# An attention stage on one NeuronCore: the token selection moved beside the next image's queries, and feature squares and products spread over ScalarE and GpSimd

## The chip, the core and the metric

The kernel runs on one core of one Trainium2 chip. A core has five engines that run their own instruction streams and meet at semaphores: TensorE (PE in the profile; its weight loads are listed apart as PEld), VectorE (DVE), ScalarE (ACT), GpSimd (POOL) and SyncE (SP, which here only issues transfers). The metric is the device time of one execution in microseconds, and it is compared by the median of several executions.

## The reference, cut to what matters

The input is four images of 256 channels and 56x56 positions, in float32. A first layer (group norm and a 7x7 involution) writes `x`. The second layer treats the 3136 positions of an image as tokens of 256 numbers:

```
t = tokens(x)
# attention, 8 heads of 32:  the weight of a pair is a square, not an exponential
scores = q . k * 32**-0.5
p      = (scores + 5)**2
t      = t + proj(sum_m p[n,m] v[m] / sum_m p[n,m])
# half of the tokens go through an MLP
u      = layernorm(t)
w      = u . wr + br
pick the 1567 tokens of largest w  (ties: lower index first)
t      = t + u  and, for the picked ones,  + w * (gelu(u @ w1 + b1) @ w2 + b2)
```

Because the weight is a polynomial of second degree in `q . k`, the sum over `m` needs no 3136x3136 matrix: it is a linear function of the 528 products `k_i k_j` of a head, of the 32 `k_i` and of a constant, each summed with `v` over all tokens.

## The kernel before, in words

`conv_layer` takes the first 1890 us of the profile and is not touched. `attn_ffn_layers` follows; nearly every instruction of it passes through `InOrder` (line 849), which keeps an engine's instructions in the order in which the program issues them. The exceptions before the change are the GpSimd instructions of this function, which are issued by `nc.gpsimd` itself and may be reordered by the framework.

For each image `b` (four of them) the program does this:

- `keys(b, g)` for the two groups of four heads, `g` = 0 and 1. It goes over the tokens in 25 tiles `m` of 128. `tokens(m)` multiplies a tile of normalised tokens `xn` with the K and V weights into PSUM (`pv`), and ScalarE copies `k` twice into one of five rows buffers `ls`, and `v` into its own tile. `features(m)` makes the products: one VectorE instruction writes `phi` (128 x 4 heads x 512: `k` times `k` shifted by 0 to 15 places; shift 0 gives the squares), a second one writes the 4x16 products of shift 16 into `ls`. `add(m, phi)` multiplies `v` with `phi` and `ls` and adds up in PSUM (`accs`, `accq`). The program issues `features(m)`, then `add(m - 1)`, then `tokens(m + 3)`.
- `coefficients(b, g)`: turns the sums into matrices for the queries, in five steps (VectorE arithmetic on `accs`/`accq`, then small matmuls and transposes `pl`, `pt`, `pr`, `pd`, each read by VectorE).
- `project(b, q)`: makes the queries `qT` of a chunk `q` of 448 tokens (seven chunks in an image) and their squares `q2`.
- `queries(b)`: 7 chunks x 2 groups x 4 feature blocks = 56 steps. In a step TensorE makes products (`pg`), ScalarE squares them (`ph`), and TensorE adds up the block of the step before (`acc`). 

All else hangs on these two loops as side work: `later` is a list of Python generators, `aside()` advances each of them by one `yield`, and `run(...)` calls `aside()` after each step of `keys` or `queries`. So a generator's `yield` sets how many steps lie between two of its parts. In the list are `weigh` (denominators), `normalise(b + 1, q)` (layer norm of the next image, which fills its `xn`), `divide` and `tokens_out` (the attention output of a chunk, its layer norm into `rows`, then two GpSimd instructions of 112x1024: `uw` for the router weights and `tk` for the residual; two steps later VectorE reduces `uw` to `w`), and `select(b)`.

`select(b)` finds the 1567 largest of the 3136 weights `w`. It builds the threshold four bits at a time: `reaching` compares all weights with up to 15 trial values on VectorE (`hit`, `per`), and after a `yield` one small matmul `pn` sums over partitions; VectorE turns the result into the next digit (`good`, `digit`, `bits`, `base`). That is done nine times, then a few matmuls (`pm`, `pa`, `pb`) give each token its place, and 28 indirect transfers by GpSimd (`us`, line 1463) scatter the rows to DRAM, two a step; each of them waits for the one before. `select(b)` enters `later` when the last chunk of image `b` is done, which is in the first part of `keys(b + 1, 0)`; for the last image it runs beside the MLP (from about 3580 us).

PSUM tiles that matter: `mm` (2 buffers, for `pv` and `pg`), `acc` (2 buffers), `sm` (2 buffers, for every small matmul: `mean`, `var`, `pq`, `pu`, `pn`, `po`, and those of `coefficients` and `select`). A buffer is free again when its last reader is done.

Before the change the order between the loops is written so:

```
        later.append(project(b, 0))
        for _ in range(5):
            aside()
        run(queries(b))
```

so that `coefficients(b, 1)` and the first queries are complete before the first step of `queries(b)`.

Of the kernel before, what the change touches and what calls it, by code (L numbers as in the profile page):

```python
# [15 lines left out]
P = 128  # L16
# [845 lines left out]
def attn_ffn_layers(  # L862
# [31 lines left out]
    sm = ctx.enter_context(tc.tile_pool(name="attn_sm", bufs=2, space=PSUM))  # L894

    inner = ctx.enter_context(ExitStack())
    xnp = inner.enter_context(tc.tile_pool(name="xn", bufs=2))
    kp = inner.enter_context(tc.tile_pool(name="k", bufs=3))
    php = inner.enter_context(tc.tile_pool(name="phi", bufs=2))
    cp = inner.enter_context(tc.tile_pool(name="coef", bufs=2))  # L900
    stp = inner.enter_context(tc.tile_pool(name="sums", bufs=1))
    qp = inner.enter_context(tc.tile_pool(name="q", bufs=2))
    ve, te, se, sy = (
        InOrder(tc, e) for e in (nc.vector, nc.tensor, nc.scalar, nc.sync)
    )

    par = const.tile([P, len(COLS)], F32, name="apar")
# [54 lines left out]
        lss.append(ls)  # L962

    QUARTERS = [slice(h * DH, (h + 1) * DH) for h in range(4)]
    xns, held, later = {}, {}, []

    def load(b, q, tag):
        t = tp.tile([P, 2, CH], F32, tag=tag, name=f"{tag}{b}_{q}")
# [5 lines left out]
    def normalise(b, q):  # L974

        t = load(b, q, "t")
        yield
        p = sm.tile([P, 512], F32, tag="sm", name=f"mean_{b}_{q}")
        for c in range(2):
            te.matmul(p[:, :CH], mean_w, t[:, c], start=c == 0, stop=c == 1)  # L980
        xc = xns[b][:, :, q * CH : (q + 1) * CH]
        ve.tensor_tensor(xc, t, p[:, :CH].unsqueeze(1).to_broadcast([P, 2, CH]), ALU.subtract)
        sq = lnp.tile([P, 2, CH], F32, tag="sq", name=f"sq_{b}_{q}", bufs=1)
        se.activation(sq, xc, AF.Square)
        yield

        n = CH // 4
        p = sm.tile([P, 512], F32, tag="sm", name=f"var_{b}_{q}")
        for c in range(2):
            for j, r in enumerate(QUARTERS):  # L990
                te.matmul(
                    p[r, :n], mean_w[:, :DH], sq[:, c, j * n : (j + 1) * n],
                    start=c == 0, stop=c == 1, skip_group_check=True,
                )
# [24 lines left out]

    def keys(b, g):  # L1020

        xn = xns[b]
# [26 lines left out]
        def features(m):  # L1049

            mn = size(m)
            ls, k = lss[m % NKV], ks.pop(m)
            phi = php.tile([P, 4, NF], F32, tag="phi", name=f"phi_{b}_{g}_{m}")
            ve.tensor_tensor(
                phi[:mn].rearrange("p h (l e) -> p h l e", e=DH),
                k.unsqueeze(2).to_broadcast([mn, 4, HALF, DH]),
                further(ls[:mn, :, HALF : HALF + DH], HALF), ALU.mult,
            )
            ve.tensor_tensor(
                ls[:mn, :, :HALF], k[:, :, :HALF], ls[:mn, :, DH : DH + HALF], ALU.mult  # L1060
            )
            return phi

# [115 lines left out]
    def project(b, q):  # L1179

        f = slice(q * CH, (q + 1) * CH)
        qT = qp.tile([P, 2, CH], F32, tag="qT", name=f"qT_{b}_{q}")
        q2 = qp.tile([P, 2, CH], F32, tag="q2", name=f"q2_{b}_{q}")
        held["q", b, q] = qT, q2
        for g in range(2):
            p = sm.tile([P, 512], F32, tag="sm", name=f"pq{g}_{b}_{q}")
            for c in range(2):
                te.matmul(
                    p[:, :CH], wqkv[:, c, g * P : (g + 1) * P], xns[b][:, c, f],
                    start=c == 0, stop=c == 1,  # L1190
                )
            ve.tensor_scalar(qT[:, g], p[:, :CH], col(f"q_{g}"), SCALE, ALU.add, ALU.mult)
            nc.gpsimd.tensor_tensor(q2[:, g], qT[:, g], qT[:, g], ALU.mult)  # L1193
            yield

    def weigh(b, q, g):
# [114 lines left out]
    def tokens_out(b, q, both):  # L1311

        t = load(b, q, "tr")
        if q == 0:
            held["rows", b] = slp.tile([TB, NTB, ROW_N], F32, tag="rows", name=f"rows_{b}")
            held["w", b] = slp.tile([TB, NTB], F32, tag="w", name=f"w_{b}", bufs=2)
        rows = held["rows", b][:, q * 4 : q * 4 + 4]
        u = rows[:, :, :C]
# [40 lines left out]
        nc.gpsimd.tensor_tensor(uw, u, wr.to_broadcast([TB, 4, C]), ALU.mult)  # L1359
        nc.gpsimd.tensor_tensor(tk, tk, u, ALU.add)  # L1360
        yield
        yield
        w = held["w", b][:, q * 4 : q * 4 + 4]
# [3 lines left out]
            out[b, q * CH : (q + 1) * CH].rearrange("(j p) c -> p j c", p=TB), tk  # L1367
        )
        if q == NCH - 1:
            later.append(select(b))  # L1370

    def select(b):

# [6 lines left out]
        def reaching(values, n, at):  # L1380

            hit = slp.tile([TB, 15, NTB], F32, tag="hit", name=f"hit_{b}_{at}")
            ve.tensor_tensor(
                hit[:, :n], w.unsqueeze(1).to_broadcast([TB, n, NTB]),
                values.unsqueeze(2).to_broadcast([TB, n, NTB]), ALU.is_ge,
            )
            per = slp.tile([TB, 15], F32, tag="per", name=f"per_{b}_{at}", bufs=2)
            ve.tensor_reduce(per[:, :n], hit[:, :n], AX.X, ALU.add)
            yield
            held["reaching"] = count(n, f"pn{at}")  # L1390
            te.matmul(held["reaching"], ones, per[:, :n], start=True, stop=True)

# [4 lines left out]
        base = small(1, "base", I32)  # L1397
        yield from reaching(zero, 1, "sign")
        ve.tensor_scalar(base, held.pop("reaching"), float(TOPK), -1.0, ALU.is_lt, ALU.mult)
        yield  # L1400
        for i, shift in enumerate(SHIFTS):
            n = 15 if i else 7
            tried = slp.tile([TB, 15], I32, tag="tried", name=f"tried_{b}_{i}", bufs=2)
            ve.tensor_tensor(
                tried[:, :n], digits[:, i, :n], base.to_broadcast([TB, n]), ALU.bitwise_xor
            )
            yield from reaching(tried.bitcast(F32)[:, :n], n, i)
            good = slp.tile([TB, 15], F32, tag="good", name=f"good_{b}_{i}", bufs=2)
            ve.tensor_scalar(good[:, :n], held.pop("reaching"), float(TOPK), None, ALU.is_ge)
            digit = slp.tile([TB, 1], F32, tag="digit", name=f"digit_{b}_{i}", bufs=2)  # L1410
            ve.tensor_reduce(digit, good[:, :n], AX.X, ALU.add)
            bits = slp.tile([TB, 1], I32, tag="bits", name=f"bits_{b}_{i}", bufs=2)
            ve.tensor_scalar(bits, digit, float(1 << shift), None, ALU.mult)
            ve.tensor_tensor(base, base, bits, ALU.bitwise_xor)
            yield
        least = base.bitcast(F32)

        def standing(of, name):
# [7 lines left out]
            te.matmul(p, before, of, start=True, stop=False)  # L1426
            te.matmul(p, sums, before[:NTB, :NTB], start=False, stop=True)
            held["standing"] = p

        more, equal = small(NTB, "more"), small(NTB, "equal")  # L1430
        ve.tensor_scalar(more, w, least, None, ALU.is_gt)
# [3 lines left out]
        yield  # L1435
        p = count(1, "pm")
        te.matmul(p, ones, per, start=True, stop=True)
        room = small(1, "room")
        ve.tensor_scalar(room, p, -1.0, float(TOPK), ALU.mult, ALU.add)
        yield  # L1440
# [19 lines left out]
        ve.tensor_scalar(own_at, number, float(b * HW), None, ALU.add)  # L1460
        yield
        for m in range(NTB):
            nc.gpsimd.indirect_dma_start(  # L1463
                us[b], bass.IndirectOffsetOnAxis(ap=to[:, m : m + 1], axis=0), rows[:, m], None
            )
            if m % 2:
# [6 lines left out]
        for _ in steps:  # L1473
            aside()

    xns[0] = xnp.tile([P, 2, HW], F32, tag="xn", name="xn_0")
    for q in range(NCH):
        f = slice(q * CH, (q + 1) * CH)
        sy.dma_start(xns[0][:, :, f], ln0.rearrange("(c p) f -> p c f", p=P)[:, :, f])
    for b in range(NB):  # L1480
        if b + 1 < NB:
            xns[b + 1] = xnp.tile([P, 2, HW], F32, tag="xn", name=f"xn_{b + 1}")
        for g in range(2):
            run(keys(b, g))
            later.append(coefficients(b, g))
            aside()
        later.append(project(b, 0))
        for _ in range(5):
            aside()
        run(queries(b))  # L1490

    inner.close()
# [54 lines left out]
    def second(i):  # L1547
# [10 lines left out]
        for m in range(0, k, 2):  # L1558
# [10 lines left out]
            for j in range(2):  # L1569
# [4 lines left out]
                nc.gpsimd.indirect_dma_start(  # L1574
                    out.rearrange("b n c -> (b n) c"),
                    bass.IndirectOffsetOnAxis(
                        ap=rows.bitcast(I32)[:, m + j, C + 1 : C + 2], axis=0
# [170 lines left out]
```

## Time and profile before

| | |
|---|---|
| median of 3 executions | 3981.64 us (3970.96 to 3990.05) |
| profiled execution | 3992.79 us, span of its instructions 3991.0 us |
| mean granted TensorE clock | 0.946 of full speed |
| TensorE busy | 3586.3 us (90%), VectorE 2653.2 us (66%), ScalarE 1872.8 us (47%), GpSimd 1805.3 us (45%) |
| first layer | 0 to about 1890 us |
| attention, images 0 to 3 | about 1890 to 3570 us |
| MLP on the picked tokens | about 3580 to 3991 us |

Instructions are named in the profile as output tile <- input tiles, with the buffers' numbers left out. Almost all carry line 849, which is the helper's; so they are told apart by their tiles. A row of the table of windows gives the busy time of each engine in a stretch (union of its instructions), the granted clock of TensorE, and the share of the transfer engines. A row of the waits names who waited, for whom, how long in total, how often and the longest. The busy time of TensorE is modelled at its ends, so that 100% busy does not mean that it ran at its peak.

### The profile page before, as it was taken

To read this page: it belongs to the slowest core of one execution; us is meant where nothing else is said; L and a number is where in the kernel's file an instruction comes from. 1 tells how busy PE (TensorE), PEld (TensorE's weight loads), DVE (VectorE), ACT (ScalarE), POOL (GpSimd) and SP (SyncE) were. 2 spreads that over 40 slices of the span, in tenths; PEclk is the share of its full clock that TensorE was granted. 3 is DMA by queue.
4 is the path that set the end of the run, shared out by engine and by line. 5 is a ranking of instruction groups with operands and counts; after the bars stand their busy time and mean duration, and the time that the engine had idled before them with its cause. 6 is when DMAs were issued, how large, how long until landed. Compare 5 with 4: busy or idle time off the path is not lost.

```text
span 3991.0 us, 60965 instructions
## 1 busy us (share of the span) xinstructions
PE 3586.3 (90%) x23248; PEld 1629.9 (41%) x23248; DVE 2653.2 (66%) x3611; ACT 1872.8 (47%) x3837; POOL 1805.3 (45%) x856
## 2 busy tenths in 40 slices
PE   3989998999799999997889878998889878989998
PEld 1333333333233333332434444344434444436776
DVE  2688888899688988997954577346834576333321
ACT  2767766776477756772234412442134312442111
POOL 1568886888688978995001102111122103112231
PEclk7989999999799999998999979998899979999999
DMA  3666556664756546654002201221012201121120
GB/s 95 153 140 148 123 140 155 143 137 96 159 125 136 122 100 131 129 113 117 7 18 62 62 10 32 54 60 38 15 45 60 54 6 36 39 79 38 45 59 25
DMA packets 337515, 329.95 MB, mean 83 GB/s; under 512 B 68606, under 2 KB 327894, under 8 KB 337222
## 3 DMA queue, kind: packets, MB, share of 16 engines
q1 hardware_dynamic: 322428, 302.52, 33.9%
q0 software_dynamic: 8064, 19.48, 1.6%
q10 hardware_dynamic: 6730, 4.05, 0.4%
q8 instruction: 183, 3.00, 0.3%
q14 instruction: 110, 0.90, 0.1%
HBM read 256.77 MB, written 68.69 MB: 82 GB/s over the span
## 4 chain that ended last, share of the span: by engine, by line
PE 71%; DVE 16%; DMA 6%; issue 3%; ACT 1%; POOL 1%; SPq 1%; ACTq 0%; DVEq 0%; POOLq 0%
PE acc L849 19%; PE p L849 17%; PE pg L849 5%; DVE phi L849 5%; PE py L849 5%; PE pv L849 4%; PE ph L849 4%; PE po L849 4%; PE accs L849 3%; DVE pr L849 3%; PE z L849 3%; PE pq L849 2%; DMA xc<-x3d 1%; DVE st L849 1%; PE mean L849 1%
## 5 line engine op out<-in xcount | busy, mean ns | idle before, releaser
L849 POOL TENSOR_TENSOR pr<-xc,lg 128x1792 f32<-128x1792 f32 x280 | 1035.2, 3704 | 285.2 <-ACT lg L849 102.7
L849 PE MATMUL acc<-pr,same 128*32 128x448 f32 (+1 forms) x5824 | 682.4, 562 | 71.4 <-DVE pr L849 59.3
L849 PE MATMUL p<-y,cw 128*128 128x400 f32 (+5 forms) x1568 | 684.6, 541 | 2.4 <-ACT y L849 1.5
L849 ACT ACTIVATE ph<-pg,unit 128x896 f32<-128x896 f32 x448 | 426.8, 1004 | 462.9 <-PE pg L849 462.6
L849 DVE TENSOR_TENSOR pr<-xc,exp 128x1792 f32<-128x1792 f32 x280 | 559.4, 1998 | 54.7 <-DMA xc<-x3d 30.5
L849 DVE TENSOR_TENSOR phi<-pv,ls 128x2048 f32<-128x2048 f32 (+1 forms) x200 | 456.7, 2284 | 12.8 <-ACT v L849 10.3
L849 ACT ACTIVATE y<-p,tb,bn2s 128x200 f32<-128x200 f32 (+1 forms) x728 | 342.3, 520 | 229.4 <-PE p L849 225.2
L849 PEld LDWEIGHTS p<-y,cw 128*128 128x128 f32 (+1 forms) x1568 | 267.4, 192 | 403.1 <-issue 206.9
L849 DVE TENSOR_TENSOR pr<-xw,exp 128x1792 f32<-128x1792 f32 x168 | 338.4, 2015 | 42.3 <-issue 14.3
L849 ACT ACTIVATE ls<-pv 128x256 f32<-128x256 f32 (+1 forms) x200 | 77.5, 387 | 604.2 <-issue 510.2
L849 PE MATMUL pv<-wqkv,xn 128*128 128x256 f32 (+1 forms) x800 | 255.0, 448 | 99.5 <-DVE ls L849 73.5
L1359 POOL TENSOR_TENSOR uw<-rows,awr 112x1024 f32<-112x1024 f32 x28 | 66.0, 2359 | 601.5 <-DVE rows L849 601.5
L849 POOL TENSOR_TENSOR y<-a,ac 128x896 f32<-128x896 f32 x168 | 277.6, 1653 | 129.0 <-DMA ac<-x3d 98.0
L1463 POOL DMA_INDIRECT us<-rows,to x112 | 106.2, 948 | 487.1 <-DVE rows L849 288.9
L849 PEld LDWEIGHTS acc<-pr,same 128*32 128x32 f32 (+1 forms) x5824 | 145.5, 110 | 432.8 <-issue 245.2
L849 PE MATMUL pg<-qT,pairs 32*128 32x448 f32 x1792 | 282.5, 590 | 8.4 <-ACT ph L849 7.9
L849 PE MATMUL accs<-phi,v 128*32 128x512 f32 (+1 forms) x1600 | 235.9, 664 | 38.3 <-DVE phi L849 22.8
L1193 POOL TENSOR_TENSOR q<-qT 128x448 f32<-128x448 f32 x56 | 58.6, 1046 | 424.9 <-DVE qT L849 386.2
L849 ACT ACTIVATE lg<-p,par 128x448 f32<-128x448 f32 x392 | 233.4, 595 | 5.8 <-PE p L849 5.7
L849 PE MATMUL acc<-ph,cf 128*32 128x448 f32 (+1 forms) x1792 | 214.8, 551 | 0.0
L849 PEld LDWEIGHTS pv<-wqkv,xn 128*128 128x128 f32 (+1 forms) x800 | 153.9, 213 | 144.9 <-issue 99.7
L849 ACT ACTIVATE lg<-lg 128x1120 f32<-128x1120 f32 x168 | 163.9, 1007 | 99.1 <-DVE lg L849 98.5
(246 smaller groups left out, 5210.0 us busy)
## 6 DMA issues: line engine op xcount, KB each, us to landing
xw<-x3d SPq DMA_DIRECT2D x224, 248.0 KB
xq<-in_x SPq DMA_DIRECT2D x47, 448.0 KB
xc<-x3d SPq DMA_DIRECT2D x54, 248.0 KB
xc<-x3d SPq DMA_DIRECT2D x54, 247.0 KB
xc<-x3d SPq DMA_DIRECT2D x54, 246.0 KB
xc<-x3d SPq DMA_DIRECT2D x54, 245.0 KB
xr<-in_x SPq DMA_DIRECT2D x224, 56.0 KB
xs<-xr SPq DMA_DIRECT2D x224, 56.0 KB
```

Of the source, the lines that this page charges most:

```text
L849: return lambda *a, **k: self.tc.keep_in_program_order(of(*a, **k))
L1193: nc.gpsimd.tensor_tensor(q2[:, g], qT[:, g], qT[:, g], ALU.mult)
L1359: nc.gpsimd.tensor_tensor(uw, u, wr.to_broadcast([TB, 4, C]), ALU.mult)
L1463: nc.gpsimd.indirect_dma_start(us[b], bass.IndirectOffsetOnAxis(ap=to[:, m : m + 1], axis=0), rows[:, m], None)
```

## The change

- `select(b)` of the first three images goes to a list `whole`, and joins `later` only when `keys(b + 1, 1)` is over. It then runs beside `queries(b + 1)`. `rows` of even images take the memory that a second `xn` had, since two of them now live at once; there is one `xn` for all images.
- In `select` a `yield` now follows each counting matmul, and the one after the arithmetic goes: matmul and reader are a step apart.
- `project(b, 0)` moves from behind the keys into `keys(b, 1)`. The five bare `aside()` calls go, so that `coefficients(b, 1)` is advanced once after the keys and then by the steps of `queries(b)`.
- `features(m)`: ScalarE writes the squares (shift 0: 4 heads x 32, so 128 of the 2048 elements of `phi` in each partition) from `ls`; VectorE's instruction covers the other 1920; GpSimd writes the 4x16 products from `ls`.
- The squares `q2` of the queries go from GpSimd to ScalarE.
- GpSimd's instructions of this function are now kept in program order (`gp`).

```diff
-    xnp = inner.enter_context(tc.tile_pool(name="xn", bufs=2))
+    xnp = inner.enter_context(tc.tile_pool(name="xn", bufs=1))
...
-    ve, te, se, sy = (
-        InOrder(tc, e) for e in (nc.vector, nc.tensor, nc.scalar, nc.sync)
+    ve, te, se, sy, gp = (
+        InOrder(tc, e) for e in (nc.vector, nc.tensor, nc.scalar, nc.sync, nc.gpsimd)
     )
...
             phi = php.tile([P, 4, NF], F32, tag="phi", name=f"phi_{b}_{g}_{m}")
+            mine = ls[:mn, :, HALF : HALF + DH]
+            se.activation(phi[:mn, :, :DH], mine, AF.Square)
             ve.tensor_tensor(
-                phi[:mn].rearrange("p h (l e) -> p h l e", e=DH),
-                k.unsqueeze(2).to_broadcast([mn, 4, HALF, DH]),
-                further(ls[:mn, :, HALF : HALF + DH], HALF), ALU.mult,
-            )
-            ve.tensor_tensor(
-                ls[:mn, :, :HALF], k[:, :, :HALF], ls[:mn, :, DH : DH + HALF], ALU.mult
+                phi[:mn, :, DH:].rearrange("p h (l e) -> p h l e", e=DH),
+                k.unsqueeze(2).to_broadcast([mn, 4, HALF - 1, DH]),
+                further(ls[:mn, :, HALF + 1 : HALF + 1 + DH], HALF - 1), ALU.mult,
+            )
+            gp.tensor_tensor(
+                ls[:mn, :, :HALF], mine[:, :, :HALF], mine[:, :, HALF:], ALU.mult
             )
...
             ve.tensor_scalar(qT[:, g], p[:, :CH], col(f"q_{g}"), SCALE, ALU.add, ALU.mult)
-            nc.gpsimd.tensor_tensor(q2[:, g], qT[:, g], qT[:, g], ALU.mult)
+            se.activation(q2[:, g], qT[:, g], AF.Square)
             yield
...
-            held["rows", b] = slp.tile([TB, NTB, ROW_N], F32, tag="rows", name=f"rows_{b}")
+            held["rows", b] = (slp if b % 2 else xnp).tile(
+                [TB, NTB, ROW_N], F32, tag="rows", name=f"rows_{b}"
+            )
...
-        nc.gpsimd.tensor_tensor(uw, u, wr.to_broadcast([TB, 4, C]), ALU.mult)
-        nc.gpsimd.tensor_tensor(tk, tk, u, ALU.add)
+        gp.tensor_tensor(uw, u, wr.to_broadcast([TB, 4, C]), ALU.mult)
+        gp.tensor_tensor(tk, tk, u, ALU.add)
...
         if q == NCH - 1:
-            later.append(select(b))
+            (later if b == NB - 1 else whole).append(select(b))
...
             held["reaching"] = count(n, f"pn{at}")
             te.matmul(held["reaching"], ones, per[:, :n], start=True, stop=True)
+            yield
...
             ve.tensor_tensor(base, base, bits, ALU.bitwise_xor)
-            yield
         least = base.bitcast(F32)
...
         te.matmul(p, ones, per, start=True, stop=True)
+        yield
         room = small(1, "room")
         ve.tensor_scalar(room, p, -1.0, float(TOPK), ALU.mult, ALU.add)
-        yield
         yield from standing(equal, "e")
...
-            nc.gpsimd.indirect_dma_start(
+            gp.indirect_dma_start(
                 us[b], bass.IndirectOffsetOnAxis(ap=to[:, m : m + 1], axis=0), rows[:, m], None
             )
             if m % 2:
...
+    xn = xnp.tile([P, 2, HW], F32, name="xn")
...
         for g in range(2):
             run(keys(b, g))
             later.append(coefficients(b, g))
             aside()
-        later.append(project(b, 0))
-        for _ in range(5):
-            aside()
+            if g == 0:
+                later.append(project(b, 0))
+        later.extend(whole)
+        whole.clear()
         run(queries(b))
```

More of the change, by code (lines that the diff above doesn't have):

```diff
@@ L964, in attn_ffn_layers @@
     QUARTERS = [slice(h * DH, (h + 1) * DH) for h in range(4)]
-    xns, held, later = {}, {}, []
+    held, later, whole = {}, [], []
     def load(b, q, tag):
@@ L980, in normalise @@
             te.matmul(p[:, :CH], mean_w, t[:, c], start=c == 0, stop=c == 1)
-        xc = xns[b][:, :, q * CH : (q + 1) * CH]
+        xc = xn[:, :, q * CH : (q + 1) * CH]
         ve.tensor_tensor(xc, t, p[:, :CH].unsqueeze(1).to_broadcast([P, 2, CH]), ALU.subtract)
@@ L1020, in keys @@
     def keys(b, g):
-        xn = xns[b]
         accs = accp.tile([P, 512], F32, tag="acc", name=f"accs_{b}_{g}")
@@ L1188, in project @@
                 te.matmul(
-                    p[:, :CH], wqkv[:, c, g * P : (g + 1) * P], xns[b][:, c, f],
+                    p[:, :CH], wqkv[:, c, g * P : (g + 1) * P], xn[:, c, f],
                     start=c == 0, stop=c == 1,
@@ L1437, in select @@
         te.matmul(p, ones, per, start=True, stop=True)
+        yield
         room = small(1, "room")
         ve.tensor_scalar(room, p, -1.0, float(TOPK), ALU.mult, ALU.add)
-        yield
         yield from standing(equal, "e")
@@ L1474, in run @@
             aside()
-    xns[0] = xnp.tile([P, 2, HW], F32, tag="xn", name="xn_0")
+    xn = xnp.tile([P, 2, HW], F32, name="xn")
     for q in range(NCH):
         f = slice(q * CH, (q + 1) * CH)
-        sy.dma_start(xns[0][:, :, f], ln0.rearrange("(c p) f -> p c f", p=P)[:, :, f])
+        sy.dma_start(xn[:, :, f], ln0.rearrange("(c p) f -> p c f", p=P)[:, :, f])
     for b in range(NB):
-        if b + 1 < NB:
-            xns[b + 1] = xnp.tile([P, 2, HW], F32, tag="xn", name=f"xn_{b + 1}")
         for g in range(2):
@@ L1573, in second @@
                 )
-                nc.gpsimd.indirect_dma_start(
+                gp.indirect_dma_start(
                     out.rearrange("b n c -> (b n) c"),
```

## The prediction

> **What bounds it now.** I read the table of windows first, cut at the first and last `phi` of each keys group and the first and last `pg` of each queries loop.
>
> ```profile
> core 0: us, PE busy (x) PEld busy (x) DVE busy (x) ACT busy (x) POOL busy (x), PEclk, DMA share, GB/s
> 1895.30:1954.20 58.90, 54.45 (x667) 28.43 (x665) 58.90 (x50) 12.72 (x46) 0.00 (x0) 1.00 0.04 13
> 1963.50:2025.80 62.30, 55.22 (x676) 29.54 (x675) 59.48 (x53) 12.14 (x44) 0.00 (x0) 1.00 0.01 2
> 2025.80:2040.40 14.60, 9.34 (x55) 5.30 (x55) 7.04 (x24) 0.00 (x0) 1.87 (x2) 0.77 0.00 0
> 2040.40:2270.50 230.10, 216.82 (x1441) 89.76 (x1442) 95.79 (x214) 114.36 (x130) 36.10 (x22) 1.00 0.23 55
> 2280.50:2380.00 99.50, 73.62 (x710) 41.05 (x710) 79.49 (x128) 12.89 (x48) 9.40 (x4) 0.83 0.08 22
> 2380.00:2393.60 13.60, 11.27 (x49) 7.41 (x50) 9.27 (x36) 1.66 (x6) 0.00 (x0) 0.50 0.00 1
> 2393.60:2462.20 68.60, 56.91 (x690) 31.17 (x688) 62.06 (x70) 12.17 (x44) 14.29 (x15) 1.00 0.09 27
> ```
>
> Image 0's first group is 25 tiles in 58.9 us, 2.36 each, with DVE busy all the time. Image 1's takes 99.5: the selection lies in it. There neither PE nor DVE is full, and PE's clock is 0.83. Queries run at 230 us with PE busy 217 and DVE 42%: room for DVE work, none for PE waits. The waits in the window 2280.5 to 2380 say who waits:
>
> ```profile
> PE pv L849 <- DVE ls L849: 17.4, 8, 2.8
> DVE good L849 <- PE pn L849: 9.2, 5, 2.6
> DVE tk L849 <- PE po L849: 7.3, 2, 3.9
> ```
>
> DVE and PE wait for each other: `good` stands right behind its matmul, and while DVE waits the next `phi` is late. Last, single rows: a keys tile on DVE, and what the moved GpSimd work costs.
>
> ```profile
> 1935.26 0.21 DVE L849 TENSOR_TENSOR ls<-pv,ls 128x64 f32<-128x64 f32 x1
> 1935.42 2.29 DVE L849 TENSOR_TENSOR phi<-pv,ls 128x2048 f32<-128x2048 f32 x1
> L849 DVE TENSOR_TENSOR phi<-pv,ls x200: 2225/2284/2293, 1895.3 to 3346.5; 128x2048 f32<-128x2048 f32 x96, 64x2048 f32<-64x2048 f32 x4
> L1193 POOL TENSOR_TENSOR q<-qT x56: 932/937/1248, 2036.2 to 3536.5; 128x448 f32<-128x448 f32 x56
> L1359 POOL TENSOR_TENSOR uw<-rows,awr x28: 2346/2356/2376, 2114.7 to 3652.5; 112x1024 f32<-112x1024 f32 x28
> L1463 POOL DMA_INDIRECT us<-rows,to x112: 938/941/1111, 2417.9 to 3841.4; - x112
> 2114.94 2.14 DVE L849 TENSOR_SCALAR inv<-inv 128x14 f32<-128x14 f32 x1
> ```
>
> **Part 1: the keys' tile.** `phi` loses 128 of 2048 elements: 2.28 - 0.14 = 2.15 us, and the 0.21 us `ls` leaves DVE. PE is then the longer: from the starts in the timeline, a tile without a wait (8+16 records of `accs`/`accq`, 4 of `pv`) repeats after about 2.29 us. So a group falls from 58.9 to 25 x 2.29 = 57.5, not to DVE's 54. ScalarE gains a square of 128 elements (`v<-pv` of that size: 0.27) beside 0.66 in 2.29: covered; uncovered it would be 200 x 0.27 = 54 us. GpSimd's product has no row: between `q2` (448 elements, 0.93) and `y` (896, 1.48) the line gives about 0.47 us for 64; bounds 0.2 (DVE's price) and 0.93. Either fits in 2.29, since `ls` is filled three tiles ahead; at 0.93 uncovered it is 186 us.
>
> [...] The trace agrees for `inv`: 2.14 us while `uw` ran, 0.16 elsewhere. Were `phi` caught so, a tile would be 2.15 + 0.47 = 2.62 us and 200 tiles lose 66 us. But `phi` reads one operand from PSUM, [...] and its 200 never exceed 2.293, the six beside `uw` or `tk` included. I take 2.29.
>
> **Part 2: keys with the selection gone.** First group of image 1, DVE: 79.5 busy + 20 idle. Out go `phi` 25 x 0.14 = 3.4, `ls` 3.4, the nine countings 10.5 (per round `tried` 0.16, `hit` 0.59, `per` 0.59, `good` to `base` 0.65), the waits for `pn`/`pnsign` 10.6 and small gaps 1. 99.5 - 29 = 70; PE alone would need 57.5 + 5 (`po`) = 63, so the waits for `po` remain. Images 1 to 3 (99.5, 101.4, 100.1): -29.5, -31.4, -30.1. GpSimd is in order now: two products stand behind `uw` and `tk` (4.7 us), a PE wait of about 1.6 us each, within PE's 7 us of slack. Second group: PE-bound at 57.5 + 3 for `pr`, `pd`: 60.5 against 62.3, 68.6, 68.7, 74.5: -1.8, -8.1, -8.2, -14. Between the groups: 9.3 in image 0, 13.6 in the others; with `project`'s two `pq` and `qT` 11: +1.7, then -2.6 three times. Image 0's first group: -1.4.
>
> **Part 3: from the keys to the first `pg`.** 14.6, 14.6, 17.0, 15.0 become about 2.5 (the last `add`): -12.1, -12.1, -14.5, -12.5. But only 5 us of the 14.6 were idle: the coefficients' matmuls (4 us) come back in the queries, and `pl` now stands in PE's queue before `pg` of step 1, waiting for `spread`, behind 5 us of DVE sums: 3 us. Queries +7 in each image.
>
> **Part 4: what the queries take on.** ScalarE gets 14 `q2` (0.6 each, like a 448-element ACTIVATE) that wait in its queue for `qT`, ahead of `ph`: bounds 0 and 14 x 1 us; ScalarE is half idle, so 0.5 (image 0) to 1.5. For images 0 to 2's selections: 16 small matmuls, 0.15 us each beyond what overlaps: 2. A count now holds one of the two `sm` buffers for a whole step, so `mean` or `pq` behind `pn` of `weigh` waits for DVE's copy: about 7 times 0.6 us = 4.5; bounds 0 and 10. Its DVE work, 17 us, fits in 135 us of idle.
>
> The costly one is GpSimd's queue. 28 scatters come two a step (8.6 us for two steps of 4.3), but each waits for the one before: the fourth image's, beside other transfers, started 3.02 us apart (3759.8 to 3841.4). In order, `uw_2` now stands behind 18 of them. Image 1 from its own times: scatters begin in step 26 at 2583.9; two, then `uw_1` and `tk_1` (moved to 2587.9) end at 2592.6; 16 more hold GpSimd to 2592.6 + 15 x 3.02 + 0.94 = 2638.8; `uw_2` ends at 2641.2. DVE's reduce of it to `w` stands in program order at 2628.8 and blocks 12.4 us, and behind it `dd` and `qT`, for which PE waits after 3 us of `pg` and `acc`: 9.5 us lost. In image 3, whose queries are faster, the same sum gives 16.4, so 13.5 lost. `uw_3`, behind the last ten, comes about in time. Bounds: 0 if a pair of steps kept up, 20 if a scatter takes 3.5.
>
> The clock adds to it. Rows: 1.00 in dense stretches, 0.50 to 0.83 in those where PE waits. [...] By the row alone I would charge the 9.5 us; [...] 11 and 15.
>
> Queries: image 0 +7.5; images 1 and 2: 7 + 1.5 + 2 + 4.5 + 11 = +26; image 3 +30.
>
> **Sum.** Image 0: -1.4 + 1.7 - 1.8 - 12.1 + 7.5 = -6. Image 1: -29.5 - 2.6 - 8.1 - 12.1 + 26 = -26. Image 2: -31.4 - 2.6 - 8.2 - 14.5 + 26 = -31. Image 3: -30.1 - 2.6 - 14 - 12.5 + 30 = -29. Together -92; the first layer's order is the same, and the MLP stage, PE-bound, keeps its selection: 0. The profiled execution took 3992.8 (span 3991.0), so 3901; the median of before lies 11 lower: 3889.
>
> **Rivals.** (a) More is won, 3825: PE outruns the stalls, since the queries hold PE 13 us idle before (230 - 217) which may absorb `pl`, `sm` and part of `w`: 92 + 37 (GpSimd stalls) + 25. For it: DVE 42% busy. Against: DVE is in order, and PE cannot pass `pn`. (b) Little is won, 3950: keys stay with DVE and PE in lockstep at 2.36 (+14), the first groups end at 76 (+18), `sm` and `q2` cost their upper bounds (+30). For it: `tk` waits stay. (c) Slower: the scatter queue. At d us a transfer the first block grows by 16 us per us, and the second by 10 after it falls behind. Per image 12.4 + 16(d - 3.02), then 10d + 5.7 - 36. At d = 4.5 that is 36 + 15, some 38 more than I charge, 115 in three images, +23: from there on it is slower by 0.5%. Single intervals of 4.4 to 4.6 us stand in the trace, but the four scatters average 2.9 to 3.0. At d = 5, 4040 us. (d) The GpSimd product costs over 2.8 us, and bounds each tile: its nearest row speaks against it.
>
> **Chances.** My sum, 3850 to 3930: 0.66. (a) below 3850: 0.14. (b) between 3930 and 3962: 0.10; nearer than that to before, all bounds against me: 0.06. (c) with (d): 0.04. A measurement here tells about 0.5%, 20 us, from no change: faster 0.66 + 0.14 + 0.10 = 0.90, same 0.06, slower 0.04. The range 3840 to 3938 leaves out about 0.1 on either side.
>
> **What would show it.** Right: groups of 57 to 61 us, and 70 for the first of images 1 to 3, at clock near 1; no `good <- pn` waits; a DVE wait `w <- POOL uw` of about 12 to 16 us once in each of the queries of images 1 to 3, which take 257, 257 and 236 us; first `pg` 2 to 3 us after the last `phi`. Wrong: `phi` over 2.2 us beside GpSimd's product, `accq` waiting for POOL in every tile, or first groups still over 80.

## The result: faster by 0.9%, less than the forecast range allowed

| | before | after |
|---|---|---|
| median | 3978.51 us (3970.96 to 3990.05, 4 executions) | 3943.07 us (3942.79 to 3944.76, 4 executions) |
| ratio | | 0.9906 [0.9888, 0.9924] |
| profiled execution | 3992.79 us, clock 0.946 | 3942.82 us, span 3940.7 us, clock 0.959 |

The direction was right and the interval lies outside "within 0.5%". The size was not: 35 us between the medians, where 92 were forecast, and 3943 us lies above the range of 3840 to 3938.

The table of windows of the changed kernel, cut as it was before (a stretch, then the busy time of each engine with its instructions, the granted clock, the transfer engines' share). The rows are image 0's two keys groups and queries, then image 1's:

```profile
core 0: us, PE busy (x) PEld busy (x) DVE busy (x) ACT busy (x) POOL busy (x), PEclk, DMA share, GB/s
1887.80:1946.60 58.80, 56.66 (x667) 29.55 (x665) 53.70 (x25) 17.98 (x71) 7.72 (x24) 0.95 0.03 11
1959.40:2019.20 59.80, 54.44 (x675) 29.28 (x672) 54.09 (x28) 17.89 (x70) 7.24 (x22) 1.00 0.01 2
2020.60:2257.30 236.70, 221.27 (x1463) 92.08 (x1459) 100.70 (x235) 119.98 (x142) 23.36 (x10) 0.99 0.21 53
2267.30:2339.60 72.30, 60.66 (x696) 33.76 (x696) 62.73 (x57) 18.32 (x73) 16.91 (x28) 0.98 0.10 30
2350.80:2412.10 61.30, 55.93 (x674) 30.57 (x672) 54.03 (x28) 17.90 (x70) 7.25 (x22) 0.97 0.01 2
2413.50:2683.30 269.80, 234.85 (x1494) 96.98 (x1495) 117.72 (x312) 118.91 (x141) 51.08 (x38) 0.94 0.22 59
```

The row of before for image 1's queries:

```profile
2476.80:2708.30 231.50, 219.77 (x1441) 90.69 (x1442) 94.65 (x214) 112.97 (x129) 45.57 (x32) 0.99 0.24 58
```

Read it in pairs. Image 1's first keys group fell from 99.5 to 72.3 us and its clock rose from 0.83 to 0.98. The first `pg` now follows 1.4 us after the last `phi` (2412.1 to 2413.5), where 14.6 us lay. But image 1's queries, which took 231.5 before, now take 269.8, while image 0's, in which no selection runs, went from 230.1 to 236.7 only. Over the four images, in us:

| | image 0 | image 1 | image 2 | image 3 |
|---|---|---|---|---|
| first keys group, before and after | 58.9, 58.8 | 99.5, 72.3 | 101.4, 72.4 | 100.1, 72.6 |
| second keys group | 62.3, 59.7 | 68.6, 61.3 | 68.7, 59.8 | 74.5, 60.5 |
| last `phi` to first `pg` | 14.6, 1.4 | 14.6, 1.4 | 17.0, 1.4 | 15.0, 1.4 |
| queries | 230.1, 236.7 | 231.5, 269.8 | 231.1, 269.0 | 206.5, 243.3 |
| sum with the stretch between the groups (forecast) | -6 (-6) | -12 (-26) | -16 (-31) | -21 (-29) |

That is -55. The MLP stage, counted from its first `ft`, grew from 402.8 to 414.5, so +12, where 0 was forecast. So 43 of the 50 us between the two profiled executions are the change's. The other 7 are not: in the profile of before the first layer, which nothing touches, ended 7.5 us later (first `phi` at 1895.3 against 1887.8; the experiments below had it between 1879.1 and 1890.2).

The wait that the forecast named is in the waits of that last window (who waited for whom: us in total, times, longest):

```profile
PE pn L849 <- DVE dd L849: 22.7, 7, 14.2
...
DVE w L849 <- POOL uw L849: 15.2, 2, 14.7
```

VectorE waits 14.7 us in one piece for GpSimd's `uw`, TensorE then 14.2 us for VectorE's `dd`. It is one stall at one place, step 37 (the steps of a queries loop are counted from 0), and images 2 and 3 have it too: DVE waits 14.6 and 16.7 us. GpSimd's own timeline around it (start, duration, what was idle before it) shows why:

```profile
2598.07 0.94 POOL L849 DMA_INDIRECT us<-rows,to  x1 [1.92 <-DMA us<-rows,to]
2599.03 2.35 POOL L849 TENSOR_TENSOR uw<-rows,awr 112x1024 f32<-112x1024 f32 x1
2601.33 2.34 POOL L849 TENSOR_TENSOR tk<-tk,rows 112x1024 f32<-112x1024 f32 x1
```

`uw` starts the moment the last of 16 scatters ahead of it is issued. Each of these waits for the transfer before, the shortest intervals being 2.8 us. The 16 took from 2549.50 to 2598.07: 3.24 us each.

The MLP stage has a second such stall. Its row in the waits of that stage, before and then after:

```profile
PE ft L849 <- DMA frows<-us: 11.7, 1, 11.7
```

```profile
PE ft L849 <- DMA frows<-us: 20.5, 2, 12.2
```

The second wait, 8.36 us, is for image 2's last picked rows (`frows`), whose read comes late. Image 3's scatters, which run at that time, took from 3701.0 to 3806.4, 3.9 us apart, where they had been 3.0 apart. Again GpSimd's timeline, and behind it the read in the chain of work that ended last:

```profile
3796.54 0.94 POOL L849 DMA_INDIRECT us<-rows,to  x1 [1.92 <-DMA us<-rows,to]
3797.78 0.94 POOL L849 DMA_INDIRECT out<-fy,frows  x1 [0.30 <-issue]
3801.12 0.94 POOL L849 DMA_INDIRECT out<-fy,frows  x1 [2.40 <-DMA out<-fy,frows]
```

```profile
3803.79 2.78 DMA frows<-us
```

Results (`out`) and selected rows (`us`) now alternate in pairs in one queue, in the order of the program, and the second of each pair waits for the first to land. The read starts when the result scatter of 3801.12 has landed, at 3803.65: `frows` has three buffers, and this scatter was the last to use the one that the read fills.

### The profile page after: what moved, and what is told of

Its sections match the earlier page's. It is cut to its first block, busy times and chain, and to the rows that moved or that the text cites. A ratio compares the mean times of both kernels' runs of the same rounds, so it can differ in the third digit from the quotient of the medians.

```text
span 3940.7 us, 61459 instructions
## 1 busy us (share of the span) xinstructions
PE 3537.7 (90%) x23248; PEld 1595.4 (40%) x23248; DVE 2609.8 (66%) x3411; ACT 1945.4 (49%) x4093; POOL 1812.5 (46%) x1000
## 4 chain that ended last, share of the span: by engine, by line
PE 65%; DVE 13%; DMA 12%; issue 4%; POOL 4%; SPq 1%; ACT 1%; ACTq 0%; DVEq 0%; POOLq 0%
PE acc L849 17%; PE p L849 17%; DMA us<-rows,to 6%; PE pv L849 4%; PE accs L849 4%; PE pg L849 4%; PE py L849 4%; DVE pr L849 3%; PE po L849 3%; PE ph L849 3%; PE z L849 3%; DVE phi L849 2%; PE pq L849 2%; DMA xc<-x3d 1%; DVE st L849 1%
## 5 line engine op out<-in xcount | busy, mean ns | idle before, releaser
L849 DVE TENSOR_TENSOR phi<-pv,ls 128x1920 f32<-128x1920 f32 (+1 forms) x200 | 428.6, 2152 | 32.5 <-PE accs L849 21.0
L849 POOL TENSOR_TENSOR ls<-ls 128x64 f32<-128x64 f32 (+1 forms) x200 | 65.4, 331 | 487.1 <-ACT ls L849 487.1
L849 PE MATMUL pv<-wqkv,xn 128*128 128x256 f32 (+1 forms) x800 | 230.6, 413 | 43.3 <-DVE phi L849 19.7
L849 PE MATMUL accs<-phi,v 128*32 128x512 f32 (+1 forms) x1600 | 217.1, 614 | 26.5 <-DVE phi L849 23.9
L849 ACT ACTIVATE h<-ph,apar 128x448 f32<-128x448 f32 (+1 forms) x128 | 68.4, 586 | 299.4 <-PE ph L849 298.7
```

The lines of the kernel that those rows point to most:

```text
L849: return lambda *a, **k: self.tc.keep_in_program_order(of(*a, **k))
```

## The experiments

The theory after the result: the roughly 50 us that the stages miss are GpSimd's queue, now in program order, at two places (the queries of images 1 to 3, and the MLP). The rivals: VectorE's order, with the selection's work ahead of what TensorE waits for; and PSUM, since a counting matmul now holds an `sm` buffer for a step. Each run below was timed against the kernel before on the same chip (its medians lay between 3981.3 and 3981.6; beside the changed kernel it took 3978.5, so differences from the changed kernel are uncertain by some 3 us).

**1. One scatter a step (images 0 to 2).** The change is otherwise whole.

```diff
-            if m % 2:
+            if m % 2 or b < NB - 1:
                 yield
```

> The changed kernel with the scatters of images 0 to 2 issued one in a step instead of two (28 steps of about 4.5 us, so that each 2.9 us transfer is over before the next is issued). Theory, GpSimd's queue: in the changed kernel uw of the third chunk stands behind 18 scatters, VectorE blocks 14.7, 14.6 and 16.7 us on it, and the step of the queries in which that falls takes 19.7, 19.6 and 21.9 us instead of about 4.5; here these steps are ordinary again and the time falls by 45 to 50 us against the changed kernel, to about 3895. Rival, that the stall only fills time which PE would wait anyway for the counting work: it falls by under 15 us, and the queries of image 1 stay near 265 us instead of about 254.

Measured: 3885.91 us, 0.9761 [0.9745, 0.9778], 57 us less than the changed kernel. Image 1's queries in its table of windows:

```profile
2406.90:2660.10 253.20, 232.15 (x1498) 96.74 (x1495) 118.09 (x312) 118.64 (x141) 50.36 (x38) 0.96 0.24 62
```

269.8 became 253.2, and images 2 and 3 fell to 250.5 and 223.8. `w <- uw` is gone from the waits, since GpSimd now reaches `uw` with time to spare; the row's bracket says that it waits for its input, not for a transfer:

```profile
2572.33 2.35 POOL L849 TENSOR_TENSOR uw<-rows,awr 112x1024 f32<-112x1024 f32 x1 [6.46 <-DVE rows L849]
```

Step 37 takes 3.7 us again, where it took 19.7. So the queue alone cost 55 us in the three queries, where 37 had been charged for it.

**2. The MLP's transfers out of the program order.** Image 3's `us` and all `out` scatters go by `nc.gpsimd`, as before the change.

```diff
-            gp.indirect_dma_start(
+            (nc.gpsimd if b == NB - 1 else gp).indirect_dma_start(
                 us[b], ...
...
-                gp.indirect_dma_start(
+                nc.gpsimd.indirect_dma_start(
                     out.rearrange(...), ...
```

> The changed kernel, but the scatter of image 3 and the MLP's own scatters to the output are issued without the program order on GpSimd, as before the change. Theory: the MLP stage became 12 us longer (402.8 to 414.5 us from its first transpose) because image 3's scatter is interleaved in order with output scatters, ends 105 instead of 82 us after its start, and the fetch of the first part of image 3 comes late (an 8.4 us PE gap at 280.6 us into the stage); here the gap goes and the time falls by 10 to 13 us against the changed kernel. Rival: the gap comes from the selection's three additional yields, not from the queue; then the time stays within 3 us.

Measured: 3931.66 us, 0.9875 [0.9859, 0.9892], 11 us less than the changed kernel. The MLP takes 405.7 us, 9 of the 12 us less, the scatters run 3.1 us apart, and the waits have one entry again:

```profile
PE ft L849 <- DMA frows<-us: 11.9, 1, 11.9
```

Most of the loss of the MLP stage is therefore the order of two kinds of transfers in one queue. The expectation took the late read for the first part of image 3; it is the last part of image 2, held up as told above.

**3. The selection behind the other side work of a step.** If VectorE's order mattered, it should gain.

```diff
     def aside():
-        later[:] = [s for s in later if next(s, held) is not held]
+        for steps in (later, last):
+            steps[:] = [s for s in steps if next(s, held) is not held]
...
-        later.extend(whole)
+        last.extend(whole)
```

> The changed kernel with the selections of images 0 to 2 advanced after all other side work of a step instead of before it, so that VectorE's counting instructions stand behind dd and qT in its queue. Theory, order on VectorE: besides the 15 to 18 us block, the queries of images 1 to 3 are 15 us longer than those of image 0 because about 2 us of counting stands ahead of dd and PE's pn waits for dd (8.5 us in image 1 without the long block) and qT is late for ScalarE; here those waits go and the time falls by 20 to 30 us. Rival, the held sm buffer: a count's PSUM buffer is still held from one step to the next, mean and pq still wait, and the time stays within 8 us.

Measured: 3963.38 us, 0.995 [0.9932, 0.9967], 20 us more than the changed kernel. The theory falls. The early steps did come sooner (step 17 of image 1's queries starts 76.6 us into them, not 80.6), but by step 23 the lead is gone (113.0 and 112.9 us). VectorE's timeline there (start, duration):

```profile
2501.82 2.04 DVE L849 TENSOR_SCALAR inv<-inv 128x14 f32<-128x14 f32 x1
...
2504.37 1.80 DVE L849 TENSOR_TENSOR base<-base,bits 112x1 int32<-112x1 int32 x1
```

Both take 0.14 to 0.16 us when nothing is beside them. `uw` ran on GpSimd from 2501.49 and `tk` from 2503.80 to 2506.15: each VectorE instruction ends where GpSimd's does, at 2503.86 and 2503.84, then at 2506.17 and 2506.15. `inv` is caught like this beside `uw` in other kernels too (2.15 us in the paced one, 2.14 in the one before); new here is that the selection's last round stands behind it and is caught once more, beside `tk`. TensorE then waits:

```profile
2506.82 0.33 PE L849 MATMUL pm<-permore,aones 112*112 112x1 f32 x2 [2.18 <-DVE inv L849]
...
2515.04 3.00 PE L849 MATMUL pq<-xn,wqkv 128*128 128x448 f32 x4 [1.94 <-DVE dd L849]
```

The second of these can only be a wait for a buffer, since `pq` reads nothing that `dd` writes: `pm` holds one `sm` buffer until its reader at the end of the step (`room`, at 2518.68), and `pu` holds the other until `dd` has read it. There are three such waits in each of the three queries, 3.5 us together, and none in the changed kernel. A second `w <- uw` wait of 6 to 7 us appears in each as well. The selection's place in a step matters, but last is the wrong one.

**4. The counting matmul and its reader in one step again,** as before the change (the `yield` after the arithmetic, none after the matmul, and the same in the placing that follows; in all four images; all else as changed).

```diff
             te.matmul(held["reaching"], ones, per[:, :n], start=True, stop=True)
-            yield
...
             ve.tensor_tensor(base, base, bits, ALU.bitwise_xor)
+            yield
```

> The changed kernel with the yields of the selection where they were: the reader of a count follows its matmul in the same step. Theory A, that a count held in PSUM for a whole step is what costs: the buffer is free again within a step, and the time falls by 5 to 12 us. Theory B, that it is VectorE's order: VectorE now waits for a count at the end of PE's queue of the step (as good waited for pn 1.5 to 2 us at a time in the keys before), with dd and qT behind it, nine times and a few more in each of three images: the time rises by 20 to 45 us.

Measured: 3928.31 us, 0.9859 [0.9835, 0.9883], 15 us less than the changed kernel. VectorE now waits for the matmul, in the queries of image 1 by its waits

```profile
DVE good L849 <- PE pn L849: 10.2, 5, 3.2
```

and the kernel is still faster. In exchange the waits of `mean` and `pq` for `dn`, which are waits for an `sm` buffer, are gone from those queries; in the changed kernel they read

```profile
PE pq L849 <- DVE dn L849: 1.2, 3, 0.4
...
PE mean L849 <- DVE dn L849: 1.2, 3, 0.4
```

These two rows are too small to be the whole gain. Step 23, just past the countings, started 112.9 us into the queries in the changed kernel and 106.1 here. In the stretch up to it, 3.8 us of the difference are idle time of TensorE (12.9 to 9.1) and 2.7 are busy time, at clock 0.92 in the one and 0.95 in the other. Whether the short waits lower the clock is not shown. The long wait for `uw` stays (14.1, 15.1 and 19.4 us), as it should.

**5. Paced, with the countings of images 0 to 2 left out.** A constant takes the threshold's place after as many empty steps; so the first 1567 tokens of these images go through the MLP, whatever their weights.

```diff
+        if b < NB - 1:
+            least = small(1, "zero")
+            ve.memset(least, -1e30)
+            for _ in range(18):
+                yield
+        else:
             ...
```

> The changed kernel with one scatter in a step (as e1_pace), and with the nine countings of images 0 to 2 left out: a constant takes the threshold's place after as many empty yields, so that all tokens count as picked and the first 1567 tokens go through the MLP; placing and scatter stay. With e1_pace the queries of images 1, 2, 3 took 253, 251 and 224 us, those of image 0 237. Theory, that the rest of what the queries lost is the countings (nine matmuls of about 0.4 us of PE each, held sm buffers, dd behind 2 us of counting on VectorE, half-rate clock in the gaps): images 1 and 2 come to 237 to 242 us, and the time falls by 30 to 42 us against e1_pace, to about 3850. Rival, that placing, scatters and the transfers of the other queues cost it: the time falls by under 15 us.

Measured: 3863.93 us, 0.9692 [0.9667, 0.9717], 22 us less than the paced kernel: between the two expectations. The queries fall by 8.8, 9.4 and 7.1 us, to 244.4, 241.0 and 216.7, nearly all of it within the first 20 steps. Image 1's row:

```profile
2415.60:2660.00 244.40, 226.72 (x1480) 94.39 (x1477) 103.28 (x253) 118.62 (x141) 50.77 (x38) 0.97 0.26 64
```

TensorE is busy 5.4 us less than in the paced kernel's row above (232.15), with 18 instructions fewer. So the nine rounds cost some 8 us an image where I had 6.5 for matmuls and buffers; and what the queries still hold above their length before, some 10 to 13 us, is not countings.

**6. Paced, with the queries' squares on GpSimd again** (now in program order).

```diff
-            se.activation(q2[:, g], qT[:, g], AF.Square)
+            gp.tensor_tensor(q2[:, g], qT[:, g], qT[:, g], ALU.mult)
```

> e1_pace with the squares q2 of the queries on GpSimd again (in program order there). Prediction's step: q2 on ScalarE costs 0.5 us in image 0 and 1.5 us in the others, so 4 to 5 us come back and the time is 3880 to 3884. Rival: the move was needed, since in GpSimd's ordered queue q2 stands behind scatters and behind uw and tk and acc waits for it: slower than e1_pace by 5 us or more.

Measured: 3893.27 us, 0.977 [0.9742, 0.9798], against 0.9761 [0.9745, 0.9778] for the paced kernel. The intervals lie over each other: this cannot be told from no difference. The medians lean towards the rival (7 us slower); but of the 11.8 us between the two profiled executions, 4.8 lie in the first layer, and only 4.4 in the four queries. Either way, the move to ScalarE is not where time was lost.

**7 and 8. The two halves of the change, each alone.** The first is the kernel before with the squares of `phi` on ScalarE and the 64 products on GpSimd, and nothing else; the second the changed kernel with both back on VectorE.

```diff
+            mine = ls[:mn, :, HALF : HALF + DH]
+            se.activation(phi[:mn, :, :DH], mine, AF.Square)
             ve.tensor_tensor(
-                phi[:mn].rearrange(...)
+                phi[:mn, :, DH:].rearrange(...)
...
-            ve.tensor_tensor(
+            nc.gpsimd.tensor_tensor(
                 ls[:mn, :, :HALF], ...
```

> The kernel before with one part of the change alone: squares of the features by ScalarE, 4x16 products by GpSimd. Theory, that keys are bound by PE at about 2.3 us a tile and that VectorE's 0.35 us per tile is worth little where nothing else stands on VectorE, but counts where the selection does: image 0's groups fall by 0 to 2 us, first groups of images 1 to 3 by 5 to 8 us, and the whole by 15 to 35 us. Rival, that PE sets the pace everywhere: under 8 us.

> The changed kernel with one part undone: squares and 4x16 products are on VectorE again. Theory: the keys go back to 2.36 us a tile, and the first groups of images 1 to 3 from 72 to about 78 us since the attention output's VectorE work is not covered; together 15 to 35 us slower than the changed kernel, 3960 to 3978. Rival, that PE bounds the keys once the selection is gone: within 8 us of the changed kernel.

Measured: the features alone 3948.96 us, 0.9911 [0.9886, 0.9937], which is 33 us off and within the 15 to 35 expected; the scheduling alone 3985.5 us, 1.0012 [0.9999, 1.0024]. So the features give by themselves about what the whole change gives, and the rescheduling as it was written gives nothing that can be told from zero. From the other end, taking the features out of the changed kernel costs 42 us, more than the 15 to 35 expected; in the profiles 31 of it lie in the eight keys groups. Their tables of windows show image 1's first keys group, the features alone first:

```profile
2273.60:2368.70 95.10, 69.81 (x710) 39.99 (x710) 73.61 (x104) 18.10 (x73) 17.15 (x28) 0.89 0.08 23
```

```profile
2273.30:2349.00 75.70, 62.29 (x696) 34.23 (x696) 68.23 (x82) 12.72 (x48) 9.37 (x4) 0.95 0.10 29
```

The group's 27 us are the scheduling's for the most part (99.5 to 75.7; the features then take 3.4 more, and 3.4 and 5.6 in images 2 and 3). What the scheduling wins here it gives back: its queries of image 1 take 267.8 us, like those of the changed kernel.

**9 and 10. Both repairs, and with the old place of the yields.** The edits of 1 and 2 together; then those of 1, 2 and 4.

> Both GpSimd queue repairs in one: one scatter in a step for images 0 to 2 (e1_pace), and no program order between image 3's scatter and the MLP's output scatters (e2_mlp). If the two are separate, 57 + 11 us below the changed kernel: about 3875. If one only uncovers the other: above 3882.

> e10_pace_mlp with the yields of the selection where they were before (as e4_yields). e4_yields was 15 us below the changed kernel, but it also moves the scatters by some steps. Theory, that the held count in PSUM costs by itself: again 10 to 15 us, about 3862. Rival, that in e4_yields it was the place of the scatters: within 4 us of e10_pace_mlp.

Measured: 3877.78 us, 0.9744 [0.9724, 0.9765], and 3862.69 us, 0.9705 [0.9681, 0.973]. The queue repairs together bring 65 us over the changed kernel (57 and 11 each alone), the yields 15 us more, as they did without the repairs. So it was not the place of the scatters that made the difference in experiment 4. Image 1's queries in the tables of windows of the two, in that order:

```profile
2408.70:2663.20 254.50, 232.25 (x1494) 96.70 (x1495) 118.20 (x312) 118.65 (x141) 50.97 (x38) 0.96 0.24 62
```

```profile
2410.90:2658.50 247.60, 228.83 (x1498) 95.92 (x1495) 117.98 (x312) 118.74 (x141) 50.29 (x38) 0.97 0.25 64
```

VectorE is busy for the same 118 us in both: the work is the same, and only its place differs. Here VectorE's order can be told from the buffer. In images 2 and 3 TensorE's waits for `dd` are much the same with either place of the yields (8.5 and 8.2 us, 2.3 and 1.9), while its waits for `dn` go from 2.4 and 1.2 us to none. The held buffer is therefore the cause that is left. About half of what the queries lose (6.9, 6.6 and 4.5 us) is busy time of TensorE, whose clock rises by about 0.01 in each (0.96 to 0.97 in image 1); how waits of so few us come to that is not shown. The yields of the placing moved along with those of the countings and are not shown apart.

The last kernel is the best of those that compute the whole: 80 us below the changed kernel and some 119 below the one before.

## Why the prediction was right and wrong

The direction was right, and so was the place of the largest loss. Three sizes were not: the stall behind the scatters (37 us charged in three images, 55 measured), the MLP stage (0 charged without a look at its queue, 12 measured), and the countings with the rest of the queries (about 12 more than charged). In order:

**The keys' tile: right.** The rows that answer those of before (count, then duration in ns minimum/median/maximum):

```profile
L849 POOL TENSOR_TENSOR ls<-ls x200: 318/329/422, 1884.9 to 3258.3; 128x64 f32<-128x64 f32 x96, 64x64 f32<-64x64 f32 x4
L849 DVE TENSOR_TENSOR phi<-pv,ls x200: 2093/2157/2159, 1887.8 to 3260.9; 128x1920 f32<-128x1920 f32 x96, 64x1920 f32<-64x1920 f32 x4
L849 ACT ACTIVATE phi<-ls x200: 297/316/321, 1889.3 to 3260.0; 128x128 f32<-128x128 f32 x96, 64x128 f32<-64x128 f32 x4
```

`phi` takes 2.157 us (2.15 forecast), the square 0.32 (0.27), the product on GpSimd 0.33 (0.47 forecast). That forecast rested on a misread row: `y` takes 1.94 us for 896 elements in the kernel before, and 1.48 is its shortest for 672. The line through the right row gives under 0.1 us, too little: here a line through instructions of 448 and 896 elements did not price one of 64. `phi` never exceeds 2.159, whatever GpSimd does beside it; twelve of the 200 ran beside `uw` or `tk`, in the kernel before too (not six). So the choice to believe the row, and not the worst case of a 2.62 us tile, held. `phi` has one input in SBUF and one in PSUM; `base` and `inv`, with all operands in SBUF, were caught (1.80 and 2.04 us in experiment 3, against 0.14 to 0.16). Whether the place of the operands decides that was not shown apart.

Image 0's first group, forecast at 57.5 (25 tiles of 2.29 us are 57.3), seems not to have shrunk: 58.9 to 58.8. But it ran at clock 0.95, and before at 1.00; with the same keys it takes 57.0 at a clock of 0.99 to 1.00 in experiments 2, 5 and 9. Likewise the first groups of images 1 to 3 take 72.3 us at clock 0.98 in some executions and 74.5 at 0.93 in others. A difference of 2 us in one group of one execution is therefore not to be read as an effect.

**Keys without the selection: right.** 72.3 to 72.6 against 70 forecast, second groups 59.7 to 61.3 against 60.5. No wait of `good` for `pn` is left, and the waits for `po` stay as they were said to. In the window of image 1's first group:

```profile
DVE tk L849 <- PE po L849: 7.6, 2, 3.9
...
PE pv L849 <- DVE phi L849: 5.1, 3, 2.2
```

**From the keys to the first `pg`: right.** 1.4 us against 2.5, and the bill for it in image 0's queries is +6.6 against +7.5. `pl <- spread` is the wait that was named, 3.3 us where 3 were put down.

**The stall behind the scatters: right place, too small.** Forecast: DVE waits 12.4, 12.4 and 16.4 us, and TensorE loses 11, 11 and 15. Measured: DVE waits 14.7, 14.6 and 16.7, while step 37 takes 19.7, 19.6 and 21.9 us in place of 3.7 to 3.8. So some 16, 16 and 18 were lost there, and without the queue the three queries are 55 us shorter. The failed step is "for which PE waits after 3 us of `pg` and `acc`: 9.5 us lost". The wait itself came out longer, since the scatters ran 3.24 us apart and not 3.02. TensorE did have its 3.4 us of work left. But when `uw` comes, VectorE first does what has piled up, down to `dd`, which the sum left out: the reduction 1.22 us, then the addition to `w`, 1.04, then `dd`, 0.67. So 14.7 - 3.4 + 2.9 = 14.2 us idle, which is the longest of the `pn <- dd` waits. The addition takes 0.23 us when nothing is beside it; here `tk` was running. Then comes the clock:

```profile
2590.10:2602.70 12.60, 0.05 (x4) 0.00 (x0) 1.25 (x2) 0.00 (x0) 6.87 (x6) 0.65 0.12 37
2602.70:2606.10 3.40, 1.76 (x10) 0.96 (x11) 2.90 (x5) 1.19 (x2) 1.94 (x2) 0.50 0.45 124
2606.10:2609.50 3.40, 3.40 (x19) 0.89 (x18) 0.77 (x2) 2.09 (x5) 0.94 (x1) 0.77 0.65 182
```

TensorE's work before the stall ends at 2590.15, and it comes back at 2604.3 at clock 0.50. In narrower windows of this trace the clock is 1.00 up to 2593.9, 0.50 from 2594.1 to 2607.5 and 1.00 again from 2607.7, some 3.3 us after TensorE is back. `pq` takes 3.09 us there and 1.67 us at clock 1.00 (at 2586.63), so 1.4 us are lost to the clock. That is about the 1.5 us by which the prediction's 11 exceeds its 9.5, which was the author's estimate: no row of before gives its size.

**The MLP at zero: wrong.** "The MLP stage, PE-bound, keeps its selection: 0" looked at the bound of the stage and not at its queue. The change puts GpSimd in program order everywhere, and I followed that only where the selection had moved. It cost 11 to 12 us: the late read of image 2's last picked rows, 8.4 us in one wait, makes up most of it.

**What the countings cost: somewhat too small.** The term was 2 + 4.5 us an image. Leaving nine rounds out takes 7 to 9.5 us off the queries. The held buffer was sized about right: some 5 us an image by experiment 10 (15 in three). The matmuls were not: 5.4 us of TensorE's busy time go with the nine rounds in image 1, 0.6 a round where 0.15 was put down for a matmul (the clock, which rises as well, from 0.96 to 0.97, is in it). What the queries hold beyond the countings is 10 to 13 us an image, where 8.5 were put down for the coefficients and `q2`; this rest is not taken apart here. The matmul a step ahead does remove VectorE's wait, but VectorE is busy for 118 of 270 us there and has no use for what it saves.

**The sum and the range.** The stages of the attention gave 55 us and not 92. Of the 37 missing, the queries make 30: the queue 18 (55 us by the paced kernel's queries, less the 37 charged) and the countings and the rest 12. The keys groups with the stretches between them make 12, of which 4 come back at the first `pg`. The MLP takes 12 more, which leaves 43. The medians show 35; the 8 us between lie within the spread of the kernel before, whose executions differ by 19 us. The range ended 49 us above the sum; that was too low since all the terms that were too small (the stall, the MLP, the countings, the keys) erred to the same side. With the queue repaired the gain over before is 104 us, and 119 with the yields where they were: what the keys give up is real, and was given back elsewhere.

**The rivals.** (c), the scatters' queue, was the right mechanism, at 3.24 us a transfer and not the 4.5 from which it would have decided. (b), little gained at 3950, came nearest in time, but by luck and for another reason: the keys did not stay in lockstep, and `q2` cost nothing that could be told. (a), below 3850, did not come: even the kernel without the stalls and with the yields where they were takes 3862.69. (d) did not come either: the product takes 0.33 us, where it named 2.8.

## What to carry to other kernels

Putting an engine's instructions into program order is a change to all that passes through its queue: list each chain of dependent transfers on it, multiply by the interval of one, and see which arithmetic stands behind. Pace serial transfers below the rate at which they complete, so that the queue is free when the next instruction is due: one a step in place of two was worth 57 us here. When a late input blocks an in-order engine, work out the loss of the engine behind it as the wait, less its slack, plus the work piled up in between (14.7 - 3.4 + 2.9 = 14.2 us here); and moving a reader away from its matmul keeps a PSUM buffer for as long: here it cost more than it gave, 15 us by experiments 4 and 10, since the reader's engine was not the short one.

## What the hardware showed that was not expected

- Indirect scatters that wait for each other never came less than 2.8 us apart in the traces of before and after (0.94 to issue, 1.9 until the next may go). The 16 ahead of image 1's `uw` came 3.24 us apart on average, with single ones at 5.2; in the four intervals among them of 3.79 us or more the transfer engines' share was 0.26 to 0.69, in the others between 0.13 and 0.42.
- A VectorE instruction on one column (112x1) took 1.80 us beside a GpSimd instruction of 2.35 us, against 0.16 alone; a 112x4 addition took 1.04 against 0.23. For these two it mattered more what ran beside them than what they do.
- A GpSimd product of 128x64 took 0.33 us, of 128x448 0.93 us: small work is no bad use of it where a tile of 2.3 us hides it.
